# Four graph layers on one core: how a block of attention gives back its sums, and how two row vectors reach all partitions

## The chip, the cores and the metric

The kernel runs on one core of a Trainium2 chip. The metric is device time in microseconds (us), the median of several runs. Engines are named as the profile names them: PE (TensorE), PEld (its weight loads), DVE (VectorE), ACT (ScalarE), POOL (GpSimd) and SP (SyncE, which here only issues DMAs).

## The reference

`x` is 4096 x 256 in float32 and `adj` is a 4096 x 4096 matrix of zeros and ones. Four layers follow one another; each adds to `x` a function of `h = relu(layernorm(x))` and `adj`. Cut to what matters:

```python
# layers 0 and 2: attention whose logit is a sum of two vectors
Wh   = h @ W
e    = Wh @ a_src + (Wh @ a_dst).T
e    = where(e > 0, e, slope * e)            # slope 0.2 in layer 0, 0.01 in layer 2
attn = softmax(where(adj > 0, e, -huge), axis=1)
# layer 0: attn @ Wh goes into a row-wise network (gates, softmax, silu, norms)
# layer 2:
x = x + elu(attn @ Wh)
# layer 1: x + (mean of h over neighbours) @ W.T + b
# layer 3: x + softmax(Q K^T, masked to neighbours and self) @ V
```

## The kernel before

**Tiles.** The 4096 rows are 32 tiles of 128 (`NT`), and four tiles make a block (`RB = 4`), so layer 2's attention has eight blocks. Layer 0 cuts its first block in two (`cuts`), so that it has nine, the first two of half size. `xs` holds all of `x` in SBUF.

**The two attentions** share the class `Attention`. In a block, the softmax weights are built transposed: neighbours on the partitions, and the block's 4 x 128 rows along the free dimension. A pair is two neighbour tiles, 16 pairs make a block. In `run`, the loop over pairs `n` does the following:

- `reach(n + 16 + LEAD)` (line 265) works ahead, for the next block, with LEAD = 5: DVE keeps the running minimum `run` (in PSUM) of the stored code minus the neighbour's logit term. This needs the code tile `turned`: in layer 0 made by PE and ACT and stored to DRAM by SP, in layer 2 loaded by SP from DRAM into one of 8 buffers (`stored`, line 909), once POOL has finished with the tile that was there.
- `logits` (line 325): DVE makes two operations of 128 x 512 for the pair (line 332), POOL subtracts the code (line 336). The result `y` has eight buffers; one is free again when PE has used it.
- three pairs later (`lag` = 3) in program order, ACT takes the exponential (line 363), and PE multiplies `y` with `v` into four sums `acc` of 128 x 257 in PSUM (line 374); float32 multiplications are two PE instructions each in the trace. Column 0 of `v` is one, so column 0 of `acc` is the softmax's denominator.
- at the last pair of a block, DVE takes four reciprocals `rden` straight from PSUM (line 382) and calls `finish`.

Layer 0 has four buffers for `acc`, layer 2 five; a block has four sums. The next block's first products need a buffer that `finish` has released.

**`top`** (line 286) runs when the next block's `run` is complete. ACT copies `run` to SBUF, PE transposes it, DVE takes the minimum and computes the two per-row numbers a and b as `ab`, with the row on the partition (128 x 2 x 4). Both are needed along the free dimension on all 128 partitions. So PE transposes `ab` (line 304), ACT copies `abT` (line 306), SP stores it to DRAM (line 319, eight rows of 512 bytes), waits, and reads it back, broadcast to all partitions, as `ab_row` (line 320, 512 KB). ACT copies the half b into PSUM when the block's first logits are built (line 330). The first three blocks of layer 0 (`spread = 3`) spread `abT` by matmul instead.

**`finish0`** (line 442) divides the sums into `xs`, two on ACT, two on DVE. **`finish2`** (line 918) makes elu: `h = sum * rden - 1`, two on ACT, two on DVE, from PSUM; `e = exp(h + 1)` on ACT; `min(e, 1) + x` and `max(h, -1) + ...` on DVE. Its tiles `hp` and `e` have one buffer each.

**Order.** The tile framework settles the order of instructions on each engine ahead of the run, from program order and its own estimate of durations, and it sets all waits. On the chip each engine takes its queue in that fixed order. A change of one operation can so move others on the same queue.

After layer 2, the preparation of layer 3 begins (lines 1142 to 1175), with `code` loads on SP (line 1200) into memory that layer 2 has given back.

Of the kernel before, what the change touches and what calls it, by code (L numbers as in the profile page):

```python
# [11 lines left out]
F32 = mybir.dt.float32  # L12
# [3 lines left out]
AF = mybir.ActivationFunctionType  # L16
ALU = mybir.AluOpType
# [4 lines left out]
P = 128  # L22
# [19 lines left out]
def kernel(ctx: ExitStack, tc: tile.TileContext, w: dict, out: bass.AP):  # L42
    nc = tc.nc
    x, adj = w["x"], w["adj"]
    N, D = x.shape
# [8 lines left out]
    RB = 4  # L54
# [137 lines left out]
    class Attention:  # L192
        def __init__(self, es, tag, slope, lag, n_y, blocks, turned, finish, ps_top=None):
            self.tag, self.slope, self.lag, self.n_y = tag, slope, lag, n_y
            self.turned, self.finish = turned, finish
# [90 lines left out]
        def top(self, b):  # L286
# [16 lines left out]
            ps = self.ps_top.tile([2 * n, P], F32, tag="top", name="abT")  # L303
            nc.tensor.transpose(ps, ab.rearrange("p v r -> p (v r)"), ident)
# [33 lines left out]
        def run(self, es, lead, n_acc, ahead=lambda n: None):  # L338
# [11 lines left out]
            for n in range(len(pairs) + LAG):  # L350
# [8 lines left out]
                if n >= LAG:  # L359
# [18 lines left out]
                    if c == NT - 2:  # L378
                        done = accs.pop(b)
                        rden = self.small.tile([P, RB], F32, tag="rden", name="rden")  # L380
                        for r, acc in enumerate(done):
                            nc.vector.reciprocal(rden[:, r : r + 1], acc[:, 0:1])
                        self.finish(self.blocks[b]["at"], done, rden)
# [46 lines left out]
    with ExitStack() as l0:  # L430
# [10 lines left out]
        with ExitStack() as es:  # L441
            def finish0(at, accs, rden):

                for r, acc in enumerate(accs):
                    dst, by = xs[:, at + r, :], rden[:, r : r + 1]
                    if r % 2:
                        nc.vector.tensor_scalar(dst, acc[:, 1 : D + 1], by, None, ALU.mult)
                    else:
                        nc.scalar.mul(dst, acc[:, 1 : D + 1], by)
# [11 lines left out]
            att = Attention(es, "l0", 0.2, 3, 8, cuts, turned_of, finish0, ps_c)  # L461
# [456 lines left out]
    def finish2(at, accs, rden):  # L918

        h = work2.tile([P, RB, D], F32, tag="hp", name="hp")  # L920
        for r, acc in enumerate(accs):
            by = rden[:, r : r + 1]
            if r % 2:
                nc.vector.tensor_scalar(
                    h[:, r, :], acc[:, 1 : D + 1], by, -1.0, ALU.mult, ALU.add
                )
            else:
                nc.scalar.activation(  # L928
                    h[:, r, :], acc[:, 1 : D + 1], AF.Identity, scale=by, bias=minus
                )  # L930
# [7 lines left out]
    att2 = Attention(l2, "l2", 0.01, 3, 8, cuts2, None, finish2)  # L938
# [414 lines left out]
```

## Time and profile before

| | us |
|---|---|
| median of 3 runs | 2993.16 (2993.07 to 2996.29) |
| the profiled execution's own time | 2988.39 |
| its span | 2986.5 |
| mean granted TensorE clock of it | 0.99 |
| layer 0's attention, from the span's start | about 62 to 620 |
| layer 0's row-wise network | 620 to 1217 |
| layer 1 | 1217 to 1490 |
| layer 2's preparation and attention | 1490 to 2012 |
| layer 3 | 2012 to the end |

The profile is one execution, and its times are us from the span's start. A group of instructions is named by line, engine, operation and by what it writes and reads, `out<-in`. A wait is given as "who waits <- whom", with total, times and longest. In the timeline the brackets at the end hold the idle time of the engine before the instruction, and what ended it. The chain that ended last is followed back from the last instruction; time on it counts, while idle time of an engine beside it does not.

### The profile page before, as it was taken

The page shows a single profiled execution, that of the slowest core. Times are in us where ns is not written, and L with a number is a line of the kernel's source. Part 1 is how long each engine was busy: PE and PEld are TensorE (multiplying, and loading weights), DVE is VectorE, ACT ScalarE, POOL GpSimd, SP SyncE. Part 2 cuts the span into 40 slices and gives each one's busy share as a digit, 9 for nine tenths or more (in the row PEclk, how much of TensorE's full clock was granted, in tenths as well). Part 3 has the DMA queues.
Part 4 walks back from the last instruction along what each step waited for, and adds up shares of the span by engine and source line. Part 5 has one row for each costly group of instructions (what it writes and reads, how often), then busy time and mean ns, then how long its engine had stood idle before and what let it go on. Part 6 is the DMA issues. An engine that isn't in the chain of part 4 may idle for free.

```text
span 2986.5 us, 35207 instructions
## 1 busy us (share of the span) xinstructions
PE 2862.8 (96%) x13381; PEld 2332.3 (78%) x13381; DVE 1906.5 (64%) x3458; ACT 1279.1 (43%) x1963; POOL 948.4 (32%) x718
## 2 busy tenths in 40 slices
PE   7989999999999999899999998999999999999999
PEld 6778888866555666788878777888888888888888
DVE  6787777435555554577689877646766566566653
ACT  6666555369996223891264333432212112111211
POOL 5576665535544333320046555540000000000000
PEclk9999999999999999999999999999999999999999
DMA  6776655144542000695342212002111111111100
GB/s 155 177 169 129 140 128 138 59 69 75 82 77 49 8 8 8 158 238 167 99 184 78 78 64 78 29 13 68 56 53 45 38 34 62 39 34 62 34 8 8
DMA packets 109161, 238.62 MB, mean 80 GB/s; under 512 B 10736, under 2 KB 31200, under 8 KB 100288
## 3 DMA queue, kind: packets, MB, share of 16 engines
q1 hardware_dynamic: 70736, 166.74, 16.2%
q0 software_dynamic: 37696, 69.11, 14.3%
q8 instruction: 105, 1.72, 0.2%
q14 instruction: 64, 0.52, 0.1%
q10 hardware_dynamic: 560, 0.52, 0.1%
HBM read 265.63 MB, written 37.81 MB: 102 GB/s over the span
## 4 chain that ended last, share of the span: by engine, by line
PE 70%; ACT 8%; DVE 7%; issue 6%; POOL 6%; DMA 3%; POOLq 0%; SPq 0%; ACTq 0%; DVEq 0%
PE acc L374 20%; PE acc L1285 15%; PE s L154 15%; PE mm L154 9%; PE acc L1017 8%; POOL y L336 3%; ACT sign L180 3%; DVE y L332 2%; DVE run L280 1%; PE cT L495 1%; DMA turned<-codesT 1%; PE q_ps L154 1%; ACT t L710 1%; ACT y L363 1%; DMA a<-in_adj_dram 1%
## 5 line engine op out<-in xcount | busy, mean ns | idle before, releaser
L374 PE MATMUL acc<-v,y 128*128 128x257 f32 x4096 | 929.6, 385 | 27.2 <-ACT hp L928 16.7
L374 PEld LDWEIGHTS acc<-v,y 128*128 128x128 f32 x4096 | 775.3, 192 | 139.9 <-ACT hp L928 21.1
L336 POOL TENSOR_TENSOR y<-y,turned 128x1024 f32<-128x1024 f32 (+1 forms) x272 | 545.3, 2016 | 321.7 <-DVE y L332 267.7
L363 ACT ACTIVATE y<-y,sdst 128x512 f32<-128x512 f32 (+1 forms) x544 | 350.4, 690 | 408.7 <-POOL y L336 408.5
L332 DVE SCALAR_TENSOR_TENSOR y<-ab_row,cdst,b 128x512 f32<-128x512 f32 (+1 forms) x544 | 370.9, 710 | 137.8 <-PE acc L374 122.9
L1285 PE MATMUL acc<-v,y 128*128 128x257 f32 x2048 | 454.5, 380 | 0.4 <-DVE rden L1293 0.4
L154 PE MATMUL s<-qT,hT 128*128 128x256 f32 x2048 | 445.2, 379 | 0.7 <-ACT qT L1233 0.7
L1278 ACT ACTIVATE y<-y 128x1024 f32<-128x1024 f32 x128 | 132.2, 1055 | 714.3 <-DVE y L1277 710.1
L154 PEld LDWEIGHTS s<-qT,hT 128*128 128x128 f32 x2048 | 389.0, 190 | 54.2 <-ACT qT L1233 1.4
L1285 PEld LDWEIGHTS acc<-v,y 128*128 128x128 f32 x2048 | 387.1, 190 | 55.9 <-issue 0.8
L180 ACT ACTIVATE sign<-a,limits 128x1024 bf16<-128x1024 bf16 x256 | 293.8, 1148 | 15.5 <-DMA a<-in_adj_dram 9.9
L1247 DVE SCALAR_TENSOR_TENSOR y<-code,s 128x512 f32<-128x512 bf16 x256 | 175.7, 687 | 100.8 <-PE s L154 100.5
L280 DVE SCALAR_TENSOR_TENSOR run<-turned,v,run 128x512 f32<-128x512 bf16 (+1 forms) x279 | 193.1, 692 | 31.8 <-ACT turned L500 22.4
L280 DVE SCALAR_TENSOR_TENSOR run<-turned,dst,run 128x512 f32<-128x512 bf16 x248 | 186.5, 752 | 24.6 <-DMA turned<-codesT 20.5
L1277 DVE TENSOR_TENSOR y<-y,top 128x1024 f32<-128x1024 f32 x128 | 146.2, 1213 | 43.0 <-PE top L1271 43.0
L1254 DVE TENSOR_TENSOR mx<-mx,y 128x512 f32<-128x512 f32 x224 | 154.8, 691 | 7.5
L500 ACT ACTIVATE turned<-cT,log_wide 128x1024 bf16<-128x1024 bf16 x128 | 138.9, 1105 | 28.2 <-PE cT L495 28.1
L154 PE MATMUL mm<-kept 128*128 128x512 f32 x288 | 137.0, 613 | 1.4 <-DVE kept L698 0.8
L173 POOL DMA_DIRECT2D a<-in_adj_dram x128 | 76.6, 600 | 193.3 <-ACT sign L180 146.9
L1017 PE MATMUL acc<-early,eq 128*128 128x512 f32 x512 | 127.7, 398 | 5.1 <-issue 3.3
L1017 PE MATMUL acc<-late,eq 128*128 128x512 f32 x512 | 122.9, 391 | 0.0
L1017 PEld LDWEIGHTS acc<-early,eq 128*128 128x128 f32 x512 | 95.8, 188 | 28.6 <-issue 3.7
(233 smaller groups left out, 3009.8 us busy)
## 6 DMA issues: line engine op xcount, KB each, us to landing
turned<-codesT SPq DMA_DIRECT2D x36, 1024.0 KB, 4.8
adj_t<-in_adj_dram POOLq DMA_DIRECT2D x128, 256.0 KB, 6.0
codesT<-turned SPq DMA_DIRECT2D x32, 1024.0 KB, 5.2
a<-in_adj_dram POOLq DMA_DIRECT2D x128, 256.0 KB, 4.6
code<-codesT SPq DMA_DIRECT2D x128, 256.0 KB, 4.0
code<-codesT SPq DMA_DIRECT2D x64, 512.0 KB, 8.4
ab_row<-l_ab_d SPq DMA_DIRECT2D x14, 512.0 KB, 5.3
xs<-in_x_dram SPq DMA_DIRECT2D x8, 512.0 KB, 15.1
```

What stands on the lines that cost most here:

```text
L154: nc.tensor.matmul(out=ps, lhsT=lhsT_of(k), rhs=rhs_of(k), start=(k == 0), stop=(k == n - 1))
L180: nc.scalar.activation(sign, self.came[g], AF.Sign, bias=limits[:, v : v + 1], accum_out=over[:, t, v, q : q + 1],)
L280: nc.vector.scalar_tensor_tensor(st["run"], code, dst, st["run"], ALU.subtract, ALU.min)
L332: nc.vector.scalar_tensor_tensor(y[:, :, k, :], st["ab"][:, 0, :, :], self.cdst[:, c + k : c + k + 1], st["b"], ALU.add, ALU.max,)
L336: nc.gpsimd.tensor_tensor(y, y, mask[:, :, c % QT : c % QT + 2, :], ALU.subtract)
L363: nc.scalar.activation(y[:, :, k, :], y[:, :, k, :], AF.Exp, bias=self.sdst[:, c + k : c + k + 1],)
L374: nc.tensor.matmul(out=acc, lhsT=y[:, r, k, :], rhs=self.v[:, c + k, 0 : D + 1], start=(c + k == 0), stop=(c + k == NT - 1),)
L1017: nc.tensor.matmul(out=acc, lhsT=eqs[c // (NT // 2)][:, ts(c % (NT // 2), P)], rhs=v1[c // BT][:, c % BT, :, :], start=(c == 0), stop=(c = ...
L1247: nc.vector.scalar_tensor_tensor(y[:, :, c : c + 2, :], st["code"][:, :, c : c + 2, :], -BIG / UNIT, ps, ALU.mult, ALU.add,)
L1254: nc.vector.tensor_tensor(mx, mx, y[:, :, c : c + 2, :], ALU.max)
L1277: nc.vector.tensor_tensor(part, part, top, ALU.subtract)
L1285: nc.tensor.matmul(out=accs[r], lhsT=st["y"][:, r, c, :], rhs=v3[:, c, :], start=(c == 0), stop=(c == NT - 1),)
```

## The change

Four things change in the two attentions.

In `top`, blocks that don't spread by matmul no longer transpose `ab`. SP stores `ab` from its 128 x 2 x 4 form straight into the same DRAM rows, entry by entry (1024 entries of four bytes). The read back is as before.

At the last pair of a block, `run` asks a new function `room` for SBUF room, and ACT copies each sum there as it is, and its denominator into a tile `den`. DVE then takes one reciprocal over the four denominators from SBUF. In layer 0 the room is the rows of `xs` itself, in layer 2 the tile `hp`.

`finish0` scales the four in SBUF, all on DVE. `finish2` scales and subtracts one on ACT for all four, in SBUF. A new minimum with -1 on POOL stands ahead of the exponential, `exp(min(h, -1) + 1)`, in place of the minimum after it on DVE; the addition of the rows of `xs` goes to POOL; DVE keeps the last operation.

```diff
@@ class Attention
-        def __init__(self, es, tag, slope, lag, n_y, blocks, turned, finish, ps_top=None):
+        def __init__(self, es, tag, slope, lag, n_y, blocks, turned, room, finish, ps_top=None):
...
@@ top
-            ps = self.ps_top.tile([2 * n, P], F32, tag="top", name="abT")
-            nc.tensor.transpose(ps, ab.rearrange("p v r -> p (v r)"), ident)
-            abT = self.small.tile([2 * n, P], F32, tag="abT", name="abT_sb")
-            nc.scalar.copy(abT, ps)
             st["ab"] = self.row_p.tile([P, 2, n, P], F32, tag="ab", name="ab_row")
             if b < self.spread:
+                ps = self.ps_top.tile([2 * n, P], F32, tag="top", name="abT")
+                nc.tensor.transpose(ps, ab.rearrange("p v r -> p (v r)"), ident)
+                abT = self.small.tile([2 * n, P], F32, tag="abT", name="abT_sb")
+                nc.scalar.copy(abT, ps)
...
-            nc.sync.dma_start(out=self.ab_d[b].rearrange("v r i -> (v r) i"), in_=abT)
+            with nc.allow_non_contiguous_dma(reason="rows of a few entries"):
+                nc.sync.dma_start(out=self.ab_d[b].rearrange("v r i -> i v r"), in_=ab)
@@ run
                     if c == NT - 2:
                         done = accs.pop(b)
+                        at, n_r = self.blocks[b]["at"], self.blocks[b]["n"]
+                        den = self.small.tile([P, RB], F32, tag="den", name="den")
+                        raw = self.room(at, n_r)
+                        for r, acc in enumerate(done):
+                            nc.scalar.copy(raw[:, r, :], acc[:, 1 : D + 1])
+                            nc.scalar.copy(den[:, r : r + 1], acc[:, 0:1])
                         rden = self.small.tile([P, RB], F32, tag="rden", name="rden")
-                        for r, acc in enumerate(done):
-                            nc.vector.reciprocal(rden[:, r : r + 1], acc[:, 0:1])
-                        self.finish(self.blocks[b]["at"], done, rden)
+                        nc.vector.reciprocal(rden[:, 0:n_r], den[:, 0:n_r])
+                        self.finish(at, raw, rden)
@@ layer 0
-            def finish0(at, accs, rden):
-                for r, acc in enumerate(accs):
-                    dst, by = xs[:, at + r, :], rden[:, r : r + 1]
-                    if r % 2:
-                        nc.vector.tensor_scalar(dst, acc[:, 1 : D + 1], by, None, ALU.mult)
-                    else:
-                        nc.scalar.mul(dst, acc[:, 1 : D + 1], by)
+            def room0(at, n):
+                return xs[:, at : at + n, :]
+
+            def finish0(at, raw, rden):
+                for r in range(raw.shape[1]):
+                    nc.vector.tensor_scalar(
+                        raw[:, r, :], raw[:, r, :], rden[:, r : r + 1], None, ALU.mult
+                    )
@@ layer 2
-    def finish2(at, accs, rden):
-        h = work2.tile([P, RB, D], F32, tag="hp", name="hp")
-        for r, acc in enumerate(accs):
-            by = rden[:, r : r + 1]
-            if r % 2:
-                nc.vector.tensor_scalar(
-                    h[:, r, :], acc[:, 1 : D + 1], by, -1.0, ALU.mult, ALU.add
-                )
-            else:
-                nc.scalar.activation(
-                    h[:, r, :], acc[:, 1 : D + 1], AF.Identity, scale=by, bias=minus
-                )
+    def room2(at, n):
+        return work2.tile([P, RB, D], F32, tag="hp", name="hp")
+
+    def finish2(at, h, rden):
+        for r in range(RB):
+            nc.scalar.activation(
+                h[:, r, :], h[:, r, :], AF.Identity, scale=rden[:, r : r + 1], bias=minus
+            )
         e = work2.tile([P, RB, D], F32, tag="e", name="e")
-        nc.scalar.activation(e, h, AF.Exp, bias=ones[:, 0:1])
+        nc.gpsimd.tensor_scalar(e, h, -1.0, None, ALU.min)
+        nc.scalar.activation(e, e, AF.Exp, bias=ones[:, 0:1])
         rows = xs[:, at : at + RB, :]
-        nc.vector.scalar_tensor_tensor(e, e, 1.0, rows, ALU.min, ALU.add)
+        nc.gpsimd.tensor_tensor(e, e, rows, ALU.add)
         nc.vector.scalar_tensor_tensor(rows, h, -1.0, e, ALU.max, ALU.add)
```

More of the change, by code (lines that the diff above doesn't have):

```diff
@@ L192 @@
     class Attention:
-        def __init__(self, es, tag, slope, lag, n_y, blocks, turned, finish, ps_top=None):
+        def __init__(self, es, tag, slope, lag, n_y, blocks, turned, room, finish, ps_top=None):
             self.tag, self.slope, self.lag, self.n_y = tag, slope, lag, n_y
-            self.turned, self.finish = turned, finish
+            self.turned, self.room, self.finish = turned, room, finish
             self.blocks = [{"at": at, "n": n} for at, n in blocks]
@@ L460 @@
             ps_c = es.enter_context(tc.tile_pool(name="ps_c", bufs=2, space=PSUM))
-            att = Attention(es, "l0", 0.2, 3, 8, cuts, turned_of, finish0, ps_c)
+            att = Attention(es, "l0", 0.2, 3, 8, cuts, turned_of, room0, finish0, ps_c)
             att.hold(v0, "right")
@@ L916 @@
     nc.gpsimd.memset(minus, -1.0)
-    def finish2(at, accs, rden):
-        h = work2.tile([P, RB, D], F32, tag="hp", name="hp")
-        for r, acc in enumerate(accs):
-            by = rden[:, r : r + 1]
-            if r % 2:
-                nc.vector.tensor_scalar(
-                    h[:, r, :], acc[:, 1 : D + 1], by, -1.0, ALU.mult, ALU.add
-                )
-            else:
-                nc.scalar.activation(
-                    h[:, r, :], acc[:, 1 : D + 1], AF.Identity, scale=by, bias=minus
-                )
+    def room2(at, n):
[5 more added lines that the diff above has]
+            )
         e = work2.tile([P, RB, D], F32, tag="e", name="e")
-        nc.scalar.activation(e, h, AF.Exp, bias=ones[:, 0:1])
+        nc.gpsimd.tensor_scalar(e, h, -1.0, None, ALU.min)
+        nc.scalar.activation(e, e, AF.Exp, bias=ones[:, 0:1])
         rows = xs[:, at : at + RB, :]
-        nc.vector.scalar_tensor_tensor(e, e, 1.0, rows, ALU.min, ALU.add)
+        nc.gpsimd.tensor_tensor(e, e, rows, ALU.add)
         nc.vector.scalar_tensor_tensor(rows, h, -1.0, e, ALU.max, ALU.add)
     cuts2 = [(t, RB) for t in range(0, NT, RB)]
-    att2 = Attention(l2, "l2", 0.01, 3, 8, cuts2, None, finish2)
+    att2 = Attention(l2, "l2", 0.01, 3, 8, cuts2, None, room2, finish2)
     one2 = l2.enter_context(tc.tile_pool(name="l2_one", bufs=1))
```

## The prediction

> **What bounds it now.** I read the busy table first, then the chain that ended last, then TensorE's waits in the two stages that run the changed code (layer 0's attention, about 62 to 620 us of the span, and layer 2's, 1524 to 2012), and last the timeline at one block end.
>
> ```profile
> PE 2862.8 (96%) x13381; PEld 2332.3 (78%) x13381; DVE 1906.5 (64%) x3458; ACT 1279.1 (43%) x1963; POOL 948.4 (32%) x718
> ...
> PE 70%; ACT 8%; DVE 7%; issue 6%; POOL 6%; DMA 3%; POOLq 0%; SPq 0%; ACTq 0%; DVEq 0%
> ```
>
> TensorE (PE) is busy 96% of the span and 70% of the ending chain, so only time in which PE stands still can be won. The waits of PE alone, first from 170 to 640 us (layer 0), then from 1520 to 2020 us (layer 2); columns are total, times, longest:
>
> ```profile
> PE acc L374 <- ACT xs L449: 8.5, 6, 2.9
> PE abT L304 <- DVE ab L302: 7.8, 6, 1.4
> ```
> ```profile
> PE acc L374 <- ACT hp L928: 16.7, 10, 5.2
> PE abT L304 <- DVE ab L302: 11.1, 7, 2.1
> ```
>
> The reader is to see two kinds of stall, 44.1 us together, and the change touches both. `abT` is the little transpose of a and b: PE meets it in its queue before VectorE (DVE) has written `ab`, and stands. `acc` at a block's end waits for the previous block's sums to leave PSUM. Why that is up to 5.2 us shows in the timeline of one boundary (start, duration, engine, line):
>
> ```profile
> 1764.51 0.75 DVE L278 TENSOR_SCALAR run<-turned,dst 128x512 f32<-128x512 bf16 x1 [4.59 <-DMA turned<-codesT]
> ...
> 1768.73 0.16 DVE L382 RECIPROCAL rden<-acc 128x1 f32<-128x1 f32 x1
> ...
> 1768.93 0.56 ACT L928 ACTIVATE hp<-acc,minus,rden 128x256 f32<-128x256 f32 x1 [4.92 <-DVE rden L382]
> ...
> 1769.54 0.70 PE L374 MATMUL acc<-v,y 128*128 128x257 f32 x2 [3.99 <-ACT hp L928]
> ```
>
> The sums were finished near 1765.5. Their release hung on a reciprocal, queued on DVE behind a `reach` operation that waited 4.59 us for a code load. A release by ScalarE (ACT) alone, which had been idle since 1764.0, does not pass that queue.
>
> **What the Trainium skill says.** (1) "DMA: Bandwidth & Descriptors", section "Rules for kernel authors": a last dimension that isn't contiguous becomes one descriptor per element. The new store is 1024 entries of 4 bytes. The trace agrees in direction: the column load `c_b_hz` (1024 entries, 4 KB) landed after 4.0 us, `c_abp_b` (256 entries) after 2.5. (2) "GPSIMD Engine Reference", section "Engine selection": two-input elementwise work is about 2 times slower on GpSimd (POOL) than on VectorE. Here an add of 128x1024 takes POOL 2.35 us (L873) and DVE 1.21 when undisturbed (L935). (3) "SBUF — State Buffer", section "Who interferes with whom": a DVE instruction with two SBUF inputs contends with a POOL one that reads SBUF. The trace agrees: L934 takes 1.21 to 3.04 us, median 2.43. So the elementwise moves relieve DVE by more than their bare time.
>
> **The change, part by part.**
>
> *a and b without the transpose.* 14 of 17 `abT` transposes go (6 in layer 0, 8 in layer 2; blocks 0 to 2 of layer 0 keep theirs). PE loses the waits 7.8 + 11.1 = 18.9 us, and 14 slots of 0.11 us (1614.92 to 1615.03) = 1.5. Gain 20.4. ACT loses 14 copies of 0.24 us.
>
> *The store entry by entry.* SP's row read (L320) waits for the store: 1.25 us now (1615.51 to 1616.77). New store: below, 1.25 as now; above, 12.4, the longest landing of a code load, for a store caught in such traffic; I take 4.0 from `c_b_hz`. From `ab` to the store 0.74 us is saved, so the row comes some 2 us later. Behind it on SP stand code loads (layer 2) and code stores (layer 0). ACT's copy `b` (L330) waits for the row, and the next block's `y` on DVE and POOL wait for ACT. The cover, at the worst block:
>
> ```profile
> 1741.32 0.32 SPq L912 DMA_DIRECT2D turned<-codesT  x1
> ...
> 1741.73 0.38 SPq L320 DMA_DIRECT2D ab_row<-l_ab_d  x1
> ...
> 1747.32 0.59 ACT L330 COPY b<-ab_row 128x512 f32<-128x512 f32 x1 [4.66 <-DMA ab_row<-l_ab_d]
> ...
> 1752.20 1.33 ACT L363 ACTIVATE y<-y,sdst 128x512 f32<-128x512 f32 x2 [4.29 <-POOL y L336]
> ```
>
> PE needs that first exponential only at the block end, 1765.5: 13 us of cover, and L320 stood behind a load until 1741.7 anyway. Cost 0; without the cover, each us late costs one per block. At layer 2's first block the store meets eight code loads: 0 to 4 us, I take 1.
>
> *The release.* ACT copies each 128x256 sum from PSUM: 0.365 us alone (L1024), 0.26 in a row (two L254 copies took 0.62). The 128x1 copy is in no row; below 0.1 (the overlap of two copies), above 0.24 (`abT` copy, 8x128); I take 0.15. So 0.4 to 0.6 us per sum, against 0.44 us that PE takes to finish the next (two instructions of 0.22). ACT can keep pace: sum 0 is free 0.6 us after its end, when PE is still busy for 1.3 us with the other three. An ACT exponential under way (0.7 to 1.4 us) may delay it. I put 0.5 us per boundary in place of 8.5/6 and 16.7/7: 25.2 - 13 × 0.5 = 18.7 us gained; bounds 10 and 25.
>
> *Layer 0's scaling.* DVE: one reciprocal for four (-0.49 us), four SBUF multiplies of 0.32 (DVE's L631) for two from PSUM of 0.48: +0.3, less 0.49, about nothing; ACT loses two of 0.465. DVE stood 78.7 us waiting for PE in `y` here: covered.
>
> *Layer 2's finish, off the release path.* Per block ACT gets four Identity operations (2.08 us, as L134 x4) for two of 0.555; DVE loses about 1.45 us of reciprocals and `hp` and 1.2 to 3.0 of L934. POOL gets a minimum, 2.4 us (estimate from 1.56 at 512 and 1.16 at 256 elements, L808 and L631), and an add, 2.35. POOL then has 274 + 8 × 4.75 = 312 us of 488. New waits: ACT's Exp waits for POOL's minimum; behind it stand the next exponentials. POOL's add waits for Exp; behind it stand the next `y`. DVE's last step waits for the add. End to end: 2.0 + 0.2 + 2.1 + 2.4 + 1.1 + 2.4 + 1.2 = 11.4 us, plus up to two `y` (2.13 each) that POOL is in. At 1764.0 ACT had some six pairs ready, 6 × 3.52 = 21 us of PE work. Covered: 0.
>
> *Does DVE deliver?* Blocks 3 to 5 of layer 2 (1644 to 1838) ran 62, 64 and 68 us though PE needs 56.3; DVE was busy 51 to 53 there, waited 7 to 11 for code loads and only 1 to 4 for PE. DVE sets its own pace there, and PE lives on the reserve. By 1838 PE would come some 21 us earlier (24 us of stalls less residue). DVE comes about 5 × 3 = 15 us earlier, less 1 per block for the row, so 10 to 15. The 13 us of cover shrink to 2 to 7. I take 5 us of starvation, bounds 0 and 15.
>
> *Seams.* After layer 2's last block the chain above ends about 5 us later than the 6.4 us it takes now (2010.96 to 2017.3). SP's code load L1200 waits for it (4.1 us now), and ACT's copies of `wqT` stand behind the Identities. +3, bounds 0 and 6. Layer 0's end: +0.5.
>
> **Sum.** -20.4 - 18.7 + 5 + 1 + 3 + 0.5 = -29.6 us. Against the profiled execution, 2988.4 us (span 2986.5 and 1.9 around it), that is 2958.8. The median shown, 2993.2, is 4.8 higher; against it 2963.6. I forecast 2964.
>
> **Rivals.**
>
> *The supply of `y` binds.* Layer 2's gain goes into starvation: bound 15 instead of 5, and another 5 of code loads that SP issues after a longer store. For it: DVE's own pace in blocks 3 to 5. Against: DVE loses work, and blocks 7 and 8 leave it 20.5 and 12.4 us of waiting for PE. -29.6 + 15 = about -15: 2978.
>
> *Nothing comes of it.* The two stages are held by loads and by DVE, and both stalls return elsewhere in PE's queue. 2993. Against: layer 0 has no such sign.
>
> *Slower: the finish chain holds up ACT.* The order on each engine is fixed beforehand. If ACT meets the first Identity or the Exp before DVE and POOL can answer, all exponentials wait. The chain of 11.4 + 4.3 us of `y` = 15.7, with a code load of 5 us ahead of the reciprocal 20.7, stands against a reserve of 13 to 21 us. What it outlasts the reserve by is lost at seven boundaries, against 39.1 gained less 4.5 at seams and start, so it decides from a reserve under 20.7 - 34.6 / 7 = 15.8 us. At 13 us it is 7 × 7.7 - 34.6 = +19: 3012. Against: the order before put the reciprocals just where PE ended (they waited for `acc` 2.5 us in all over the first seven ends of layer 2).
>
> *The change may not do what it says* only where the `abT` wait merely moves to the next matmul, which then waits for exponentials; that is the second rival.
>
> **Chances.** Forecast 0.58, supply binds 0.21, nothing 0.08, slower 0.13. Within 0.2% (6 us) is about what a measurement of this kernel can tell from no change. Faster 0.79, same 0.08, slower 0.13. The likeliest case alone spans 2952 to 2973: bounds of the release (-6, +9), the starvation (-5, +10) and the seams, not all at once. The range goes on to 2994 to take in the two cases above it; what is left out is the slower rival and a little below.
>
> **What would show it.** Right: in PE's waits no `abT` from layer 2, `acc` on ACT under 8 us in both stages, a few us of `acc` on `y`; layer 2 about 20 us and layer 0 about 14 us shorter; `l_ab_d` landing 3 to 6 us. Wrong: `acc` waiting tens of us on ACT's `y` exponentials, with ACT's Exp waiting for POOL's minimum or ACT's `b` for the row; or layer 2 still at 62 us and more per block in its middle.

## The result, and the profile after

The changed kernel takes **3138.8 us** (median of 5 runs, 3133.71 to 3139.16), beside 2993.16 of the kernel before: a ratio of 1.0479, interval [1.0465, 1.0493]. It is slower by 145.6 us, and the forecast said 29.6 faster. The span of the profiled execution is 3137.0 us, 150.5 more than before. Line numbers have moved: `acc` is L376, ACT's `b` L332, the store L321, the row read L322, the copies of the sums L387 and of the denominators L388.

The busy table and the chain that ended last, of the kernel after:

```profile
PE 2902.1 (93%) x13367; PEld 2362.8 (75%) x13367; DVE 1890.6 (60%) x3403; ACT 1301.6 (41%) x2077; POOL 986.0 (31%) x734
...
PE 61%; DMA 9%; DVE 8%; ACT 7%; issue 7%; POOL 6%; SPq 1%; POOLq 0%; DVEq 0%; ACTq 0%
```

PE has 14 instructions fewer, the transposes, and yet is busy 39.3 us longer; it stands 111.2 us longer (3137.0 - 2902.1 = 234.9, before 123.7). DMA's share of the chain has grown from 3% to 9%: more of the chain now consists of transfers. PE's waits, first from 170 to 700 us (layer 0), then from 1600 to 2170 us (layer 2); columns are total, times, longest:

```profile
PE cT L504 <- ACT turned L509: 37.5, 6, 9.3
PE acc L376 <- issue: 24.4, 6, 5.9
PE acc L376 <- ACT den L388: 1.4, 2, 1.2
```
```profile
PE acc L376 <- ACT den L388: 81.0, 14, 11.4
```

No `abT` is left, as foreseen. But layer 2 has one wait of about 10 us at each block end, for the sums of the block before, where it had 16.7 us in all. In layer 0 PE meets transposes of the codes (`cT`) that wait for ACT's `turned`, and `acc` stands 24.4 us under "issue". These six waits are at the block ends too, and PE goes on there just after ACT has copied the first denominator:

```profile
566.91 0.16 ACT L388 COPY den<-acc 128x1 f32<-128x1 f32 x1
...
567.17 5.27 PE L376 MATMUL acc<-v,y 128*128 128x257 f32 x16 [5.91 <-issue]
```

So I read them as waits for the sums as well, which the view doesn't name. Why the waits come up shows in one block of layer 2, in the timeline of SP, DVE, ACT and PE:

```profile
1709.86 0.15 DVE L302 SCALAR_TENSOR_TENSOR ab<-v,m 128x4 f32<-128x4 f32 x1
...
1710.04 0.37 SPq L321 DMA_DIRECT2D l_ab_d<-ab  x1
...
1720.67 0.32 SPq L322 DMA_DIRECT2D ab_row<-l_ab_d  x1
...
1725.35 0.59 ACT L332 COPY b<-ab_row 128x512 f32<-128x512 f32 x1 [9.69 <-DMA ab_row<-l_ab_d]
1725.97 2.72 DVE L334 SCALAR_TENSOR_TENSOR y<-ab_row,cdst,b 128x512 f32<-128x512 f32 x4 [10.15 <-ACT b L332]
...
1744.91 0.35 ACT L387 COPY hp<-acc 128x256 f32<-128x256 f32 x1
...
1745.37 2.08 PE L376 MATMUL acc<-v,y 128*128 128x257 f32 x4 [9.49 <-ACT den L388]
```

The row read is issued 10.6 us after the store: that is the store's landing. ACT stands 9.69 us at `b` and DVE 10.15 behind it; PE, whose sums were done at 1735.9, stands 9.49. The lateness passes through nearly undiminished. Between `b` and the release of the sums ACT has 12 exponentials, six pairs of the *next* block (from layer 2's start the trace has 64 exponentials, two whole blocks, before this `b`); from `b` to the release it takes 19.6 us. In the kernel before it was 21.6 us (1747.32 to 1768.93), in the same order. So what arrives late at `b` can delay the release by about as much; the experiments test this.

The landing time of the store in the kernel after, from its table of DMA issues (count, KB each, median us from issue to landing):

```profile
l_ab_d<-ab SPq DMA_DIRECT2D x14, 4.0 KB, 10.7
```

The 1024 entries take 10.7 us; the same 4 KB as eight rows took 1.25. The store goes out 0.74 us earlier, so a row is later by an estimated 10.7 - 1.25 - 0.74 = 8.7 us, and for 14 blocks that makes 122 us.

### The profile page after: what moved, and what is told of

The parts are those of the page before. It is cut to its first block, busy times and chain, and to the rows that moved or that the text cites. A ratio compares the mean times of both kernels' runs of the same rounds, so it can differ in the third digit from the quotient of the medians.

```text
span 3137.0 us, 35183 instructions
## 1 busy us (share of the span) xinstructions
PE 2902.1 (93%) x13367; PEld 2362.8 (75%) x13367; DVE 1890.6 (60%) x3403; ACT 1301.6 (41%) x2077; POOL 986.0 (31%) x734
## 2 busy tenths in 40 slices
DMA packets 123498, 238.62 MB, mean 76 GB/s; under 512 B 25184, under 2 KB 45536, under 8 KB 114624
## 4 chain that ended last, share of the span: by engine, by line
PE 61%; DMA 9%; DVE 8%; ACT 7%; issue 7%; POOL 6%; SPq 1%; POOLq 0%; DVEq 0%; ACTq 0%
PE acc L376 14%; PE acc L1291 14%; PE s L154 14%; PE mm L154 8%; PE acc L1023 7%; DMA l_ab_d<-ab 4%; POOL y L338 3%; ACT sign L180 3%; DVE y L334 3%; DVE run L280 2%; DMA ab_row<-l_ab_d 2%; DMA turned<-codesT 1%; PE q_ps L154 1%; PE cT L504 1%; DMA xs<-in_x_dram 1%
## 5 line engine op out<-in xcount | busy, mean ns | idle before, releaser
L376 PE MATMUL acc<-v,y 128*128 128x257 f32 x4096 | 962.8, 395 | 108.8 <-ACT den L388 82.4
L376 PEld LDWEIGHTS acc<-v,y 128*128 128x128 f32 x4096 | 799.4, 198 | 234.8 <-ACT den L388 91.4
L1291 PE MATMUL acc<-v,y 128*128 128x257 f32 x2048 | 454.5, 380 | 0.4 <-DVE rden L1299 0.4
L1291 PEld LDWEIGHTS acc<-v,y 128*128 128x128 f32 x2048 | 387.1, 190 | 55.9 <-issue 0.8
L180 ACT ACTIVATE sign<-a,limits 128x1024 bf16<-128x1024 bf16 x256 | 293.8, 1148 | 15.1 <-DMA a<-in_adj_dram 9.3
L504 PE MATMUL cT<-identb,adj_t 128*128 128x128 bf16 x1024 | 85.1, 230 | 49.8 <-ACT turned L509 41.5
L504 PEld LDWEIGHTS <-adj_t 128*128 128x128 bf16 x1024 | 72.2, 103 | 69.4 <-issue 47.0
```

The source lines that it names most:

```text
L180: nc.scalar.activation(sign, self.came[g], AF.Sign, bias=limits[:, v : v + 1], accum_out=over[:, t, v, q : q + 1],)
L376: nc.tensor.matmul(out=acc, lhsT=y[:, r, k, :], rhs=self.v[:, c + k, 0 : D + 1], start=(c + k == 0), stop=(c + k == NT - 1),)
L504: nc.tensor.transpose(ps[:, ts(i, P)], a[:, ts(i, P)], identb)
L1291: nc.tensor.matmul(out=accs[r], lhsT=st["y"][:, r, c, :], rhs=v3[:, c, :], start=(c == 0), stop=(c == NT - 1),)
```

## The experiments

Where the time lies is read by stage, from the first and last start of the `acc` products in the trace; "rest" is what follows layer 2. Each row is one execution (before: 4.8 us below its median, e10: 6.6 below). e10 and e13 have the same code in layer 2 and differ there by 3.9 us, e8 and e13 in layer 0 by 2.3, so differences of that size between two rows say nothing.

| kernel | layer 0 | between | layer 2 | rest | median, us |
|---|---|---|---|---|---|
| before | 546.9 | 906.6 | 487.2 | 974.7 | 2993.2 |
| after | 619.0 | 917.4 | 551.0 | 977.3 | 3138.8 |
| store alone (e2) | 615.1 | 913.9 | 537.4 | 974.7 | 3117.6 |
| rows again (e1) | 557.8 | 908.0 | 507.3 | 975.4 | 3025.4 |
| release alone (e3) | 555.2 | 904.0 | 496.0 | 974.6 | 3007.4 |
| row of one block before (e11) | 559.4 | 912.9 | 534.7 | 975.8 | 3062.6 |
| row of two blocks before (e12) | 559.1 | 914.8 | 523.0 | 976.0 | 3050.0 |
| before, LEAD 8 (e8) | 557.0 | 905.0 | 465.6 | 973.1 | 2979.7 |
| release alone, LEAD 8 (e10) | 551.6 | 903.6 | 473.5 | 973.1 | 2983.9 |
| 32-byte store and copy of a (e18) | 565.0 | 908.5 | 476.2 | 973.0 | 3001.3 |

The theory, after the result: the store's latency goes straight into PE's standstill at each block. The rivals: something else in the change, GpSimd's share or ScalarE's release, costs as much; or the store's packets disturb other transfers.

### The parts apart

**Everything but the store** (`e1_rows_again`): the kernel after with the transpose and the row store back.

```diff
-            with nc.allow_non_contiguous_dma(reason="rows of a few entries"):
-                nc.sync.dma_start(out=self.ab_d[b].rearrange("v r i -> i v r"), in_=ab)
+            ps = ...  # transpose of ab, copied to abT, as before
+            nc.sync.dma_start(out=self.ab_d[b].rearrange("v r i -> (v r) i"), in_=abT)
```

> The changed kernel with one part undone: ab is transposed by PE, copied by ACT and stored as eight rows of 512 bytes, as before. Release, scaling and elu stay changed. Theory A (the store of 1024 entries, 10.7 us, makes the row late; on ACT the release of the sums stands behind the copy b and six pairs of exponentials, so each us of the row's lateness is a us of PE at a block's end): 2960 to 3000 us, the abT waits back at about 19 us, acc waiting on ACT's copies under 25 us in layer 2. Theory B (the fault is ACT's eight copies per block, or POOL's share of elu in ACT's way): above 3060 us with acc still waiting about 80 us in layer 2.

3025.4 us, 1.0109 [1.0092, 1.0126]. Most of the loss is gone, but the rest of the change is itself a loss of 32 us, outside the ranges of both theories. PE's waits from 1490 to 2200 us, and DVE's in the same stretch:

```profile
PE abT L304 <- DVE ab L302: 33.2, 7, 7.1
PE acc L374 <- ACT den L386: 9.8, 7, 3.4
```
```profile
DVE xs L939 <- POOL e L938: 41.6, 8, 6.7
```

The release's wait fell (16.7 to 9.8 us), but DVE stands some 5 us per block for POOL's add, in its fixed order, `ab` comes later and PE waits 33.2 us for it, before 11.1.

**Only the store** (`e2_entries_alone`): the kernel before with the store entry by entry and no `abT`.

> The kernel before with one part of the change: ab stored entry by entry, no transpose in blocks that don't spread. Old release, old elu. Theory A: 14 rows come 10.7 - 1.25 - 0.74 = 8.7 us later, 122 us, less 20 us of abT: about 3095 us (3060 to 3140), acc waiting on ACT's hp some 80 us in layer 2. Theory B: 2970 to 3000 us.

3117.6 us, 1.0415 [1.0398, 1.0432]: +124 us. The size agrees with the 122 above partly by luck: the `abT` waits are gone here, which the expectation put at 20 us, so the late rows cost nearer 144. By the table layer 0 with six rows grew by 68.2 us and layer 2 with eight by 50.2. `acc` waits 69.4 us for ACT's `hp` in layer 2, `cT` 40.9 us for `turned` in layer 0. So the lateness costs this with the old release too, and doesn't need the release by ACT.

**b copied by DVE** (`e4_b_on_dve`): the kernel after with `nc.vector.tensor_copy` in place of `nc.scalar.copy` for `b`.

> The changed kernel with the copy of half b from the row into PSUM on DVE in place of ACT, so that nothing on ACT's queue waits for the row. Theory A: in layer 0 the waits of cT on ACT's turned (41 us) go, since ACT runs on; in layer 2 the release still stands behind exponentials whose y comes late, so acc still waits some 70 to 85 us: 3090 to 3120 us in all. If ACT's standing at the copy b is by itself the whole loss: below 3030 us. If neither matters: 3130 to 3145.

3135.1 us, 1.0475 [1.0459, 1.0491]: no effect to speak of, a miss. `cT` still waits 46.6 us for `turned`, `acc` 79.0 for `den`. DVE now stands at `b` for the row, 79.6 us from 1490 to 2200 us. So ACT's standing at that one copy is not what matters. The explanation that fits: whoever makes `b`, the first `y` and so the first exponential of the block wait for the row, and the release is queued behind six pairs of these.

**An earlier row** (`e5_lead8`): the kernel after with `LEAD` 8 and `FRESH` 11 in place of 5 and 8 (how many pairs ahead `reach` runs, and layer 0 makes its code tiles).

> The changed kernel with LEAD 8 for 5 (and FRESH 11 for 8, which that needs in layer 0): the next block's minimum, and so the store, are ready three pairs, 10.6 us of PE, earlier. The store itself is as slow as in the changed kernel. Theory A: the lateness at a block's end goes from about 10 us to 0 to 3, and with it most of acc's 81 us in layer 2 and of the cT and acc waits of 66 us in layer 0: 3000 to 3050 us. Theory B, or a store that costs by its DMA traffic: 3120 to 3145 us.

3065.7 us, 1.0244 [1.0224, 1.0263]: half of what was hoped. Layer 0 is mended (619.0 to 567.3 us), layer 2 only from 551.0 to 530.0: there `acc` still waits 62.8 us for `den`, although ACT no longer waits for the row. DVE now waits 85.2 us for code loads (`run <- turned`), 26.1 in the kernel after. A second cost had been hidden behind the first.

**The release without GpSimd's part** (`e3_release_alone`): e1 with the old elu.

```diff
-        nc.gpsimd.tensor_scalar(e, h, -1.0, None, ALU.min)
-        nc.scalar.activation(e, e, AF.Exp, bias=ones[:, 0:1])
+        nc.scalar.activation(e, h, AF.Exp, bias=ones[:, 0:1])
...
-        nc.gpsimd.tensor_tensor(e, e, rows, ALU.add)
+        nc.vector.scalar_tensor_tensor(e, e, 1.0, rows, ALU.min, ALU.add)
```

> The kernel after, with a and b again through the transpose and stored as rows, and with the old elu (ScalarE's Exp straight from the scaled sums, the minimum and the add in one VectorE instruction). What is left of the change is the release of the sums by ScalarE and the scaling in SBUF. It differs from the rows-again kernel (3025.4 us) in the elu alone. Theory A (GpSimd's part of the elu makes VectorE stand about 5 us per block, which makes ab late): VectorE no longer waits for GpSimd's add, abT waits of layer 2 fall from 33 back to 8 to 14 us, acc on den stays under 12; time 2970 to 2995. Rival B (ScalarE's eight copies and four Identities per block hold up its exponentials, whoever does the elu): 3015 to 3030, with acc on den or abT still 40 us in sum.

3007.4 us, 1.0042 [1.0027, 1.0057], between the two. GpSimd's elu costs 3025.4 - 3007.4 = 18 us; the release with its late scaling is a loss of 13 (beside 2994.4 of the kernel before in the same measurement). PE's waits from 1490 to 2200 us:

```profile
PE abT L304 <- DVE ab L302: 22.0, 7, 4.4
PE acc L374 <- ACT den L386: 9.7, 7, 3.6
```

The stall at the block end shrank by 7.0 us and the one at `abT` grew by 10.9. In layer 0 the first hardly shrank: `acc` waits 1.0 us for `den` and 6.9 under "issue" at the block ends, read as above, so 7.9 in place of 8.5. There `top` on ACT's `run_sb` went from 1.6 to 8.3 us and `abT` from 9.1 to 10.4 (62 to 640 us).

Why the release by ACT still stands for several us shows at layer 2's longest such wait:

```profile
1781.17 0.75 DVE L278 TENSOR_SCALAR run<-turned,dst 128x512 f32<-128x512 bf16 x1 [3.29 <-DMA turned<-codesT]
...
1784.98 2.12 POOL L336 TENSOR_TENSOR y<-y,turned 128x1024 f32<-128x1024 f32 x1 [4.81 <-DVE y L332]
...
1787.14 0.72 ACT L363 ACTIVATE y<-y,sdst 128x512 f32<-128x512 f32 x1 [4.23 <-POOL y L336]
...
1788.23 2.08 PE L374 MATMUL acc<-v,y 128*128 128x257 f32 x4 [3.63 <-ACT den L386]
```

ACT had copied two of the four sums by 1782.9. The other two are queued behind an exponential of the next block, which waits for POOL's `y`, which waits for DVE, which had waited for a code load. The release passes DVE's queue after all, by a longer way. And `ab` comes later for a like reason: in four blocks of layer 2 DVE stands 9.9 us in all for code loads just ahead of `ab`, before 1.1. Why the loads come late just there, no run shows.

### What the store does to layer 2

**Rows of the block before** (`e11_row_before`): the read takes `self.ab_d[max(b - 1, self.spread)]`.

> The kernel after, but each row read takes the rows that the block before stored (long landed), so it never waits for its own block's store; the values of a and b are therefore those of the block before. All 14 stores of 1024 entries are still made. Theory A (what costs is the 10.7 us for which the row read waits): PE's waits for den in layer 2 fall from 81 to under 15 us, cT on turned in layer 0 from 41 to under 10, and the time to 2985 to 3030, what is left being GpSimd's elu. Rival C (the store's packets themselves slow the code loads, the code stores and the other transfers): time stays at 3080 or above, with VectorE's waits for code loads above 60 us.

3062.6 us, 1.0226 [1.0211, 1.0241]. In layer 0 the theory holds: 559.4 us, as in e1, and `cT` on `turned` fell to 11.3. In layer 2 it does not: `den` 67.0 us, and DVE waits 86.2 us for codes. But SP still stood 62.5 us at L322, since the next block's read is queued right behind the store that it needs, and the code loads are queued behind that read. Two causes were left, hence the next.

**Rows of two blocks before** (`e12_two_before`): `max(b - 2, self.spread)`.

> The kernel after, but each row read takes the rows stored two blocks before, so that no read, wherever it stands in SP's queue, is behind a store under way; the values of a and b are those of two blocks before. All 14 stores of 1024 entries are still made. In the kernel that reads one block before (3062.6 us), ScalarE no longer waited for rows, but SP still stood 11 us behind each store at the next block's read, with layer 2's code loads behind it (VectorE waited 86 us for them). Theory A (layer 2's remainder is SP standing at the read): SP no longer waits for the store, VectorE's waits for code loads in layer 2 fall from 86 to under 35 us, layer 2 runs in 495 to 515 us instead of 535, time 3000 to 3030. Rival C (the store's 1024 packets hold up the code loads on the DMA engines): code loads land late (over 8 us instead of 4.8), VectorE still waits over 60 us for them, time 3045 or more.

3050.0 us, 1.0181 [1.0154, 1.0208]. SP waits for a store once only in layer 2; still DVE waits 74.0 us for codes. My theory A falls, rival C holds in layer 2. Its timeline, one store, the next code load on SP, and DVE's wait for it:

```profile
1645.12 0.37 SPq L321 DMA_DIRECT2D l_ab_d<-ab  x1
...
1648.74 0.32 SPq L921 DMA_DIRECT2D turned<-codesT  x1
...
1660.56 0.76 DVE L280 SCALAR_TENSOR_TENSOR run<-turned,dst,run 128x512 f32<-128x512 bf16 x1 [6.37 <-DMA turned<-codesT]
```

The load of 1 MB was issued 3.6 us behind the store and arrived 11.8 us later; the loads of `turned` in layer 2 have 4.7, 4.8 and 12.2 us as least, median and longest landing. In e1, where the row read stands ahead of the load too but the store is eight rows, the longest is 5.3. So the store of 1024 entries holds up the load. In the kernel after, DVE waits only 26.1 us for codes and the longest landing in layer 2 is 7.9: there the row is late anyway, and the second cost hardly shows.

**The store in two halves** (`e6_halves`): one store for a, one for b, 512 entries each.

> The kernel after, with the store split in two of 512 entries each, one for a and one for b, issued one after the other. If the store costs by the entry (some 10 ns each), a half lands after 5 to 6 us when alone; both together still take 10 to 12 us from the first issue, and the time stays within 15 us of 3138. If a store has a fixed price of about 10 us whatever its entries, each half takes about 10 and the row comes later or at the same time: 3130 to 3200. If the halves run beside each other on the DMA engines, the row comes about 4 us earlier and the time falls to 3070 to 3110.

3136.4 us, 1.0468 [1.0451, 1.0486]. Each half landed after 9.9 us, the first read went out 13.1 us after the first issue (205.30 to 218.39). Both were under way together, so this doesn't tell a price by the entry from a price by the store; e14 below does.

### More lead for the parts

**The release alone, LEAD 8** (`e10_release_lead8`), **the kernel before, LEAD 8** (`e8_before_lead8`), **all but the store, LEAD 8** (`e7_rows_lead8`), and **the release in layer 2 alone, LEAD 8** (`e13_release_l2_lead8`, layer 0's `finish0` as before). The common edit:

```diff
-    LEAD = 5
+    LEAD = 8
-    FRESH = 8
+    FRESH = 11
```

> As the release-alone kernel, with LEAD 8 and FRESH 11 in place of 5 and 8, so each block's row is made three pairs (some 10 us) earlier. Theory A: rows and ab are then never late; the abT waits of both layers fall under 10 us in sum, the time to 2955 to 2985. Rival D: the earlier reach only makes VectorE wait for code loads (as it did 70 us in the kernel after with LEAD 8), and the time is the release-alone kernel's or up to 20 us above it.

2983.9 us, 0.9966 [0.9957, 0.9975]. The time is in theory A's range, but the `abT` waits are 8.5 and 15.1 us, not under 10 in sum.

> The kernel before with LEAD 8 and FRESH 11 in place of 5 and 8, nothing else. The release-alone kernel gained 23 us by the same step (3007.4 to 2983.9). If the step's gain is its own (rows and ab three pairs earlier), the kernel before gains about as much: 2965 to 2980, and the release by ScalarE is worth nothing or a loss. If the release by ScalarE is what makes the earlier row pay (layer 2 went from 487 to 473.5 us), the kernel before gains little: 2988 to 2996.

**2979.7 us, 0.9948 [0.9929, 0.9967]**, the lowest median of all these kernels and 13 us below the kernel before; its interval overlaps that of e10. So most of what e10 has over the kernel before needs no part of the change. The gain lies in layer 2, 487.2 to 465.6 us, while layer 0 gives 10 back (PE's `cT` waits 16.4 us for loads of `adj_t` there, before 9.2). PE's waits there, from 1490 to 2200 us:

```profile
PE abT L304 <- DVE ab L302: 6.5, 5, 1.6
PE acc L374 <- ACT hp L928: 6.5, 7, 1.5
```

The old release, given time, stalls no longer than ACT's (6.6 us in e10), and e10's `abT` waits are 15.1 instead of 6.5. Behind both stalls were code loads: DVE waits 5.9 us for them in layer 2 here, in the kernel before 35.2.

> The release-alone kernel with LEAD 8 (2983.9 us), but layer 0's sums leave PSUM as in the kernel before (reciprocals and scaled sums straight from PSUM, by VectorE and ScalarE in turn). Theory A (the late scaling costs layer 0 some 5 us): layer 0 falls from 551.6 to 544 to 548 us, layer 2 stays at 472 to 476, time 2974 to 2981. Rival (layer 0's extra comes from its loads and not from the release): layer 0 stays at 550 to 554, time 2981 to 2987.

2987.5 us, 0.9984 [0.9973, 0.9995]; layer 0 took 554.7 us instead of 551.6. Theory A is a miss: taking the late scaling away does not shorten layer 0. The 3.1 us themselves are no more than two executions differ by.

> The rows-again kernel (all of the change but the store; 3025.4 us) with LEAD 8 and FRESH 11. It differs from the release-alone kernel with LEAD 8 (2983.9 us) in GpSimd's part of the elu alone. Theory A (VectorE standing for GpSimd's add makes the next block late; three pairs more of lead absorb it only in part): 2992 to 3005, with abT or acc waits in layer 2 of 25 us or more. Rival (with the lead, VectorE's 5 us per block lies in a reserve): 2980 to 2988.

3014.4 us, 1.0064 [1.0048, 1.008], above theory A's range and 30.5 us above e10, which differs in the elu alone. DVE waits 43.7 us for POOL's add here; more lead does not absorb it.

### A cheap store in place of the transpose

**Pieces of 32 bytes** (`e14_contig`): the 4 KB are stored as they lie in SBUF, and the row is used through a strided view.

```diff
-                nc.sync.dma_start(out=self.ab_d[b].rearrange("v r i -> i v r"), in_=ab)
+            flat = self.ab_d[b].rearrange("v r i -> (v r i)")
+            nc.sync.dma_start(
+                out=flat.rearrange("(i x) -> i x", x=2 * n), in_=ab.rearrange("p v r -> p (v r)")
+            )
...
+            st["ab"] = st["ab"].rearrange("p v r i -> p (v r i)").rearrange(
+                "p (i v r) -> p v r i", v=2, r=n
+            )
```

> The kernel after, with the same 4 KB stored in the order in which ab lies in SBUF: 8 neighbouring entries of each partition, 128 pieces of 32 bytes in place of 1024 of 4. The row is read as before, and y and b take it through a strided view (one entry in 8), so the result is the same. Theory A (the store's price goes by its pieces): it lands in 2 to 3 us, PE's waits for den in layer 2 fall from 81 to under 15 and for turned in layer 0 from 41 to under 12; no transpose of a and b is left, so the time is that of the rows-again kernel (3025) less some of its abT waits: 2985 to 3020. Rival B (a store of a few KB from 128 partitions costs some 10 us whatever its pieces): 3110 to 3150. Rival C (strided reads slow VectorE's y from 0.70 us to 1.0 or more): 3080 and above, with VectorE busy 2050 us or more.

3114.4 us, 1.0404 [1.0386, 1.0423]. The table of DMA issues, and DVE's `y` in the groups kept apart by shape (busy, mean ns | idle before):

```profile
l_ab_d<-ab SPq DMA_DIRECT2D x14, 4.0 KB, 1.4
```
```profile
L338 DVE SCALAR_TENSOR_TENSOR y<-ab_row,cdst,b 128x512 f32<-128x512 f32 x480 | 515.6, 1110 | 81.3 <-PE acc L380 45.9 <-ACT b L336 35.2
```

The same bytes from the same partitions land in 1.4 us: the 10.7 us went by the pieces. And rival C came true: `y` takes 1.11 us in place of 0.742, 480 times, +177 us on DVE, and PE waits for the sums as long as before (`acc` 81.3 us for `den` in the whole run, 82.4 in the kernel after).

**The same without GpSimd's elu** (`e15_contig_release`), **the kernel before with that store** (`e16_contig_before`), and **with LEAD 8** (`e17_contig_before_lead8`):

> As the kernel with pieces of 32 bytes, with the old elu: no transposes of a and b, release by ScalarE, a quick store. It is what the forecast of 2964 us assumed, without GpSimd's part. If the store, and what hangs on it, was the failing step: 2970 to 2995, some 10 to 25 us under the release-alone kernel (3007.4), whose abT waits of 32 us go. If the abT waits only turn into waits for the row or for exponentials: 3000 to 3015.

> The kernel before, with only the transposes of a and b replaced by the store in pieces of 32 bytes (release and elu as before). The abT waits of PE (18.9 us in both layers) and 14 slots (1.5 us) go: if nothing takes their place, 2970 to 2982; if the row's extra lateness (1 to 2 us per block) or the starvation of y takes it, 2988 to 3000.

> The kernel before with pieces of 32 bytes and LEAD 8, FRESH 11. The kernel before with LEAD 8 alone takes 2979.7 us, of which 15.9 us are abT waits. If they go without a substitute: 2958 to 2972, below every kernel so far. If they turn into other waits: 2976 to 2984.

3101.8, 3087.1 and 3080.2 us (1.0359 [1.0344, 1.0374], 1.0312 [1.0295, 1.033], 1.0287 [1.0271, 1.0302]). All three miss, `y` being as slow as in e14, and say nothing on the transposes.

**The strided view taken away** (`e18_contig_copy`, and `e19_contig_copy_lead8`): e16 and e17 with one more ACT copy per block.

```diff
                 nc.scalar.copy(st["b"], st["ab"][:, 1, :, :])
+                st["a"] = self.row_p.tile([P, RB, P], F32, tag="a", name="a", bufs=1)[:, 0 : st["n"], :]
+                nc.scalar.copy(st["a"], st["ab"][:, 0, :, :])
```

> The kernel before with the store in 128 pieces of 32 bytes and no transposes of a and b (3087.1 us), and one more ScalarE copy per block that brings a, as the copy b does for b, out of the strided row into neighbouring entries. VectorE's y reads no strided tile then. If the strided read was what cost 93 us there: y takes 0.74 us again instead of 1.11, and the time falls by 90 to 120 us. Whether the transposes' 18.9 us of waits are then gained: 2968 to 2982 if so, 2990 to 3005 if the copy of a (0.6 to 0.9 us behind b) and the row's lateness take their place.

3001.3 us, 1.002 [1.0013, 1.0027]. `y` is back at 0.742 us and 86 us return. Layer 2 is 11.0 us shorter than before (476.2), which is what its `abT` waits were. Layer 0 is 18 us longer, with `acc` waiting 24.4 us for ACT's `xs`, before 8.5. ACT's timeline there shows a cost that I had put at 0.6 to 0.9 us:

```profile
347.17 1.09 ACT L336 COPY b<-ab_row 128x512 f32<-128x512 f32 x1 [2.09 <-DMA ab_row<-l_ab_d]
348.20 1.11 ACT L340 COPY a<-ab_row 128x512 f32<-128x512 f32 x1
```

The strided copies take 2.2 us where `b` took 0.59, so the first `y` is 1.6 us later per block; for six blocks that would be 10 of the 18. The other 8 I have not settled.

> The same with LEAD 8 and FRESH 11. The kernel before with LEAD 8 alone takes 2979.7 us with 15.9 us of abT waits. If these go without a substitute: 2958 to 2972. If they turn into waits for exponentials or for the sums: 2976 to 2990.

2987.4 us, 0.9979 [0.997, 0.9989]. Layer 2 takes 461.6 us, the shortest of all, but layer 0 565.6. Slower than e8 as a whole.

## Why the prediction was wrong, point by point

**The step that failed is "The store entry by entry", in both of its halves.** The price: I took 4.0 us from a *load* of 1024 entries, issued by POOL, with 12.4 as upper bound; 10.7 was measured. The bound had it, the value taken did not. A transfer in the other direction, on another queue, was no guide; e14 shows that the pieces make the price (1.4 us for 128). The Trainium skill's rule ("DMA: Bandwidth & Descriptors", section "Rules for kernel authors") was the right place to look, and the trace agrees with it: the packets under 512 bytes rose from 10736 to 25184, by 14448, close to the 14 x 1024 = 14336 entries of the stores.

The cover: "PE needs that first exponential only at the block end, 1765.5: 13 us of cover." True for the exponential, not for what is queued behind it. The release of the old sums stands on ACT after six pairs of the new block, and PE needs *that* at the block end as well. The lines were there before: `b` at 1747.32, the release at 1768.93 waiting for `rden`, and PE at 1769.54 standing 3.99 us for it. The last exponential ahead of the release ended at 1764.0, 1.5 us before the sums: that was the cover, not 13 us. The sentence that followed, "without the cover, each us late costs one per block", was right in kind: estimated 14 x 8.7 = 122 us, measured +124 with the `abT` waits already saved.

**A cost with no step of its own:** code loads held up behind the store, 11.8 to 12.2 us instead of 4.8. I named SP's loads behind the row read, but priced only layer 2's first block. It hardly shows in the kernel after, since the row is later still, and it is some 16 to 27 us of layer 2 once the row is not: e12 and e11 stand at 523.0 and 534.7 us where e1, with both costs gone but its `abT` waits back, has 507.3.

**"Layer 2's finish ... Covered: 0"** failed for the elu. I costed POOL's minimum at 2.4 and its add at 2.35 us; they take 2.77 and 2.35, so the chain was sized nearly right; for the add the factor of about 2 of the Trainium skill ("GPSIMD Engine Reference", section "Engine selection") held, 2.35 us against DVE's 1.21. But I held it against ACT's reserve of exponentials. The engine that stood was DVE, for POOL's add, 33.1 us in the kernel after and 41.6 in e1, and its next work is `ab` and `y`. I had written "DVE's last step waits for the add" and not asked what is queued behind that step. Measured +18 us (e1 against e3), +30.5 at LEAD 8. My sum of DVE's relief was of busy time; what counted was the order.

**The release, "18.7 us gained"** failed as well. The copies were sized rightly (median 0.37 us for a sum in layer 2 and 0.17 for a denominator), and the stalls do shrink, but by 7.6 us in place of 18.7: 16.7 to 9.7 in layer 2 and 8.5 to 7.9 in layer 0. "ACT can keep pace" and "does not pass that queue" were wrong: ACT's copies stand behind or between exponentials of the next block, and these wait for POOL and DVE (e3's timeline above). Nor is it a gain in sum: e3 is 13 us slower than the kernel before. In layer 2 `abT` waits 10.9 us longer, with DVE standing for code loads ahead of `ab`; in layer 0 `top` waits 6.7 us longer for ACT's `run_sb`. Which of ACT's operations per block (eight copies and four Identities, where it had two of 0.56 us) brings this about, or whether a changed order of the queues does, is open; no run has one without the other. With LEAD 8 the loss is in layer 2: 473.5 and 477.4 us with ACT's release (e10, e13), 465.6 with the old one (e8). Layer 0 shows none (551.6 with it, 554.7 and 557.0 without).

**The transposes, "20.4 us"**: close in layer 2, 11.0 us in e18 for 12.0 forecast (11.1 of waits and 8 slots of 0.11). In layer 0 not: there e18 is 18 us longer, ten of them by the estimate from the slow copies of a and b. The rival that the `abT` wait "merely moves" may fit layer 0 better than my sum, but e18 can't tell, since its copies are slower too.

**The starvation and the seams**, 5 and 3.5 us, were small beside this. Layer 3 with its seam grew by 2.6 us; the 10.8 us between the two attentions include layer 2's first row and were not taken apart.

**The rivals.** The slower one had the wrong mechanism: the finish chain was to hold up ACT's exponentials; ACT's Exp waited 11.9 us for POOL's minimum in all, and the point of 15.8 us of reserve never decided. Among the signs named under "Wrong", "ACT's `b` for the row" came true (141.7 us, before 20.7): the sign was on the list, but no case with its price was. It should have been the slower rival: 12.4 us for the store, less 1.25 and 0.74, at 14 blocks, is 146 us. That this is also the measured loss is chance, since the release and the elu are in that.

The sum as measured, each against its own neighbour: store (less the transposes) +124, release and scaling +13, elu +18, together +155; the whole change is +145.6, so some 9 us of these overlap.

## What to carry to other kernels

A cover has to be measured to everything that stands behind the late instruction in its engine's queue, not only to its own consumer: here a release of PSUM stood twelve exponentials behind, and the slack was 1.5 us where 13 had been counted. Price a store by its pieces (here 10.7 us for 1024, 1.4 for 128), and look at what is issued after it; when a layout saves work at one end (a transpose, or 1024 pieces), ask which later instruction reads it by stride, and how often. A step moved to an idle engine costs what the sender's queue then waits for its answer (here DVE, 30 to 44 us for POOL's add). And before a release is moved to another engine, ask what stands in that engine's queue, and for whom it waits.

## What was unexpected of the hardware

- 1024 pieces of 4 bytes from SBUF to DRAM took 10.7 us, 128 pieces of 32 bytes 1.4 us, eight rows of 512 bytes 1.25 us. A load of 1 MB issued 3.6 us behind the first kind took 11.8 us instead of 4.8.
- DVE's operation for `y`, 128x512, took 1.11 us with `ab_row` read at one entry in eight, 0.742 otherwise; ACT's copy of 128x512 took 1.09 us from that tile by the same stride, 0.59 otherwise.
- With more stalls PE's own work got slower too: the granted clock was 0.964, before 0.990, and `acc` took 395 ns in the mean, before 385. The 13367 instructions took 39.3 us more than 13381 before, a quarter of the 150.5 us. In layer 0's first half (62 to 340 us) the clock was 0.92, before 0.98. In e3 sixteen products in a row took 3.69 us, and sixteen behind a stall of 2.64 us took 5.39 (at 507.21 and 513.98). So the stalls' own length is likely not the whole of their cost.
